# Moving the first image's token preparation of layer 1 into layer 0's last twelve units, and reordering the last units of layer 3

## The chip, the cores and the metric

The kernel runs on one core of one Trainium2 chip. The metric is the device time of one launch in microseconds (us). The core has a matmul engine (PE, TensorE), three engines for elementwise work (DVE is VectorE, ACT is ScalarE, POOL is GpSimd) and SP, whose queue issues the DMAs. Each engine works through a queue of its own and meets the others at semaphores. Matmul results are written to PSUM[...]; everything else is in SBUF.

## The reference

Four residual layers work one after the other on a float32 tensor of 4 images of 56 x 56 pixels and 256 channels. Ahead of each layer stands a group normalisation over 32 groups of 8 channels.

```python
x = x + L0(gn(x))   # 7x7 neighbourhood attention with zero padding, 8 heads of 32
x = x + L1(gn(x))   # attention over all 3136 tokens of an image, one head
x = x + L2(gn(x))   # 7x7 neighbourhood attention, half the heads dilated by (1, 2)
x = x + L3(gn(x))   # shifted 7x7 window attention with bias table
```

The change deals with the start of layer 1, which is this:

```python
xn = x / jnp.maximum(jnp.linalg.norm(x, axis=-1, keepdims=True), EPS)
A = jnp.einsum('bnc,cc,bmc->bnm', xn, W_adj, xn)
A = jnp.exp(5.0 * (A - jnp.max(A, axis=-1, keepdims=True)))
A = A * (1.0 - jnp.eye(n, dtype=A.dtype))
A = A / jnp.maximum(jnp.sum(jnp.abs(A), axis=-1, keepdims=True), EPS)
...
xW = jnp.einsum('bnc,dc->bnd', x, W_aff)
...
diff = rowsum * (xW + b_aff) - AxW
```

So each token is needed in two forms: scaled to unit length (for A) and multiplied by W_aff (for xW). `W_adj` is diagonal in use: einsum's `cc` takes its diagonal.

## The kernel before

All tensors lie channels first: 128 partitions hold one half of the channels, `CC` = 2 halves. The layers run one after the other, each with its own memory pools (`run`, L2213). Odd layers take their memory from the right side of SBUF, even ones from the left, so that a layer's first tiles can be loaded while the layer before still runs. A tile that takes the place of an older one waits for the older one's last users.

*Layer 0* (`layer0`, L1135) cuts each image into 8 bands of 7 rows (32 bands in all, numbered r from 0 to 31) and each band into 4 tiles, so it has 128 units, which `attend_pairs` (L1054) runs. A unit has logits on PE (L1067), a mask added on DVE (L1074) or multiplied on POOL (L1078), exponentials on ACT (L1075, L1077), sums of pairs on POOL (`both`, L1087), products on PE (`products`, L1096), and at its end a reciprocal and a scaling on DVE (`finish`, L1242 to L1249). The products of a unit run after the logits of the next one. Between logits and products stands the unit's `fill`: other work that is spread over the units by hand. In most bands it is the projection of rows of later chunks (`project_rows`, L1184: values, keys, queries); one band late comes the out projection with the residual add (`project_out`, L1266). The rows run out in band 28; bands 29, 30 and 31, the last twelve units, have only the out projections of bands 28, 29 and 30. That of band 31 follows after the last unit (L1315). The input pool `brief` (chunks of x, normalised chunks, v and also the queries q) is used until the row projections end.

Within layer 0 the order of each engine's instructions is made by a scheduler, with its own estimates of when data is there; in layer 1 PE's and DVE's order is that of the program, in layer 3 that of all four computing engines.

*Layer 1* (`layer1`, L1329) has 3136 tokens for each image: 24 tiles of 128 and a rest of 64 tokens. Its token preparation works by chunks of four tiles (`tokens`, L1361; six chunks, and a seventh for the rest): load from the stream in memory (L1372); normalise, on DVE (L945); square, on ACT (L1382); lengths, matmuls against a column of ones (L1392), then maximum on DVE (L1394), power -1/2 on POOL (L1395) and a diagonal matrix on POOL (L1403); values, x times W_aff on PE (L1414), moved out of PSUM by ACT or DVE by turns (`evac`, L956); unit length, a matmul of ones with the diagonal (L1424) and a product on DVE into `xnT` (L1426). For the rest chunk POOL also makes `xdr` (L1430). For image 0 all of that runs at the start of layer 1, by itself (`fresh`, L1662 to L1674); for the later images it runs in small steps within the attention of the image before. After it come the "rest" units (`rest_logits`, L1488, `rest_products`, L1515) and the main units (`logits`, L1445, `products`, L1547). In the rest products ACT copies half of the PSUM results into `acc` (L1485).

`layer2_ahead` (L1763) loads layer 2's weights and bias and takes the exponential of half of the bias on ACT (six steps, L1781). In the program it stands late in layer 1, but the scheduler may put it early on ACT and SP.

*Layer 3's end* (L2187 to L2207) is written out by hand. `u3` and `u4` are the last two units, `held` is the one before. `logits(w, between)` (L1014) runs `between` after POOL's product and ahead of DVE's mask. `last_row` (L2138) does the out projection of the last row of windows in two halves: it adds its own products (L2152) to x from PSUM directly (L2159). After it `unsafe` (L2236) sums the `watch` tiles (L2242), in which sums were collected through the kernel, tests them against bounds, and writes a flag (L2250), on which the program branches into a slower, safer version of itself. POOL adds reciprocals to a watch tile (`seen`, L993).

Of the kernel before, what the change touches and what calls it, by code (L numbers as in the profile page):

```python
# [24 lines left out]
FP = mybir.dt.float32  # L25
I32 = mybir.dt.int32
AF = mybir.ActivationFunctionType
# [803 lines left out]
def direct_blocks(ctx: ExitStack, tc: tile.TileContext, d: dict, watch):  # L831
# [302 lines left out]

    def layer0(early, big, pool, brief):  # L1135
        types, width = tile_types()
        xs, looks = {}, {}

        def load(r, held=xs, tag="x"):
# [8 lines left out]

        q = {(0, i): brief.tile([P, CC, BT], FP, tag="q", name="q0", bufs=6) for i in range(3)}
        for r in (3, 4, 5, 6, 0, 1, 2):  # L1150
# [5 lines left out]
        known(0, 0)  # L1156
        wv, wk, wq = (weight(big, n, C) for n in ("wv0", "wk0", "wq0"))
        late_loads()
# [25 lines left out]
        def project_rows(r):  # L1184

            b, g = divmod(r, NCH)
            xn = xns.pop(r)
            at = left(g, CH)
            v = brief.tile([P, 4, C], FP, tag="v", name="v0", bufs=1)

            def values(a):
                value_tiles(v, a, g, CH, xn, wv, bv0, vd[b])

            def keys(m):
                pm = project(wk, m * P, lambda h: xn[:, h, at:at + CH], CH)
                rows = pm.rearrange("p (r c) -> p r c", c=S)
                for i in range(NTC):
                    c0, n = key_range(*COLS[i:i + 2])
                    dst = (kE if i in (0, NTC - 1) else kI)[:, m, i // 2, 8 * g:8 * (g + 1), :]
                    nc.scalar.activation(dst, rows[:, :, c0:c0 + n], AF.Identity, bias=bk0[:, m:m + 1])  # L1200

            def queries(m):
                pm = project(wq, m * P, lambda h: xn[:, h, at:at + CH], CH)
                y = 8 * g
                while y < 8 * (g + 1):
                    i, y1 = y // TR, min((y // TR + 1) * TR, 8 * (g + 1))
                    if (b, i) not in q:
                        q[b, i] = brief.tile([P, CC, BT], FP, tag="q", name="q0", bufs=6)
                    nc.scalar.activation(q[b, i][:, m, (y - TR * i) * S:(y1 - TR * i) * S],
                                         pm[:, (y - 8 * g) * S:(y1 - 8 * g) * S],  # L1210
                                         AF.Identity, bias=qbias[:, 0, m:m + 1], scale=SCALE)
                    y = y1

            return [lambda f=f, m=m: f(m) for f in (values, keys, queries) for m in range(2)]
# [64 lines left out]
        def stream():  # L1279
# [10 lines left out]
            for r in range(NIMG * NB0):  # L1290
# [4 lines left out]
                steps.append(lambda r=r: [load(i, looks, "xs") for i in look_at.get(r + 1, [])])  # L1295
                if r:
                    at = (len(steps) + 2) // 2
                    steps[at:at] = project_out(r - 1)
# [4 lines left out]
                attns[r] = pool.tile([P, CC, BT], FP, tag="attn", name="attn0")  # L1303
                yield from spread([pair(r, t) for t in range(NTC)], steps)

        for r in range(3):
# [3 lines left out]
            if r < 2:  # L1310
                for step in project_rows(r):
                    step()
        check_sizes(pool)
        attend_pairs(pool, stream())
        for step in project_out(NIMG * NB0 - 1):  # L1315
            step()
# [11 lines left out]

    def layer1(early, big, pool, late, next_layer):  # L1329


        NB, REST = divmod(T, P)
        NC4 = NB // 4
        nonlocal m_bufs
        m_bufs = 1
        w_aff = weight(early, "waff", C)
        acc = big.tile([P, NB, C + 1], FP, name="acc")
        racc = big.tile([P, C + 1], FP, name="racc")
        xnT = big.tile([P, CC, (NB + 1) * P], FP, name="xnT")
        xw = big.tile([P, NB + 1, C + 1], FP, name="xw")  # L1340
        xdr = big.tile([P, CC, P], FP, name="xdr")
        shares = dram.tile([NIMG, (NB + 1) * P], FP, name="shares")
# [15 lines left out]
        nc.vector.tensor_scalar(offd, ident, -1.0, 1.0, ALU.mult, ALU.add)  # L1358
        nc.vector.memset(xw[:, :, C:], -1.0)

        def tokens(b, c, ps_a=ps_m):  # L1361
# [3 lines left out]
            n = m * P  # L1365
            by_dma = b > 0 and c in (0, 1, 2, NC4)
            box = {}
# [10 lines left out]
            def normal(h):  # L1378
                normalise(box["x"][:, h, :n], box["x0"][:, h, :n], known(1, b), h)
                if h:  # L1380
                    sq = box["x0"]
                    nc.scalar.activation(sq[:, :, :n], box["x"][:, :, :n], AF.Square)  # L1382
                    if b:
                        nc.gpsimd.tensor_tensor(sq[:, 0, :n], sq[:, 0, :n], sq[:, 1, :n], ALU.add)

            def lengths():
                pm, sq = ps_a(), box["x0"]
                rn = early.tile([P, 4, 1], FP, tag="rn", name="rn")
                halves = range(1 if b else CC)
                for i in range(m):  # L1390
                    for h in halves:
                        nc.tensor.matmul(pm[:, i:i + 1], lhsT=sq[:, h, i * P:(i + 1) * P], rhs=ones[:, 0:1],  # L1392
                                         start=(h == 0), stop=(h == halves[-1]))
                nc.vector.tensor_scalar_max(rn[:, :m, 0], pm[:, :m], TINY * TINY)  # L1394
                nc.gpsimd.tensor_tensor(rn[:, :m, 0], rn[:, :m, 0], mhalf[:, 0:1].to_broadcast([P, m]), ALU.pow)  # L1395
                box["share"] = early.tile([P, 4, P], FP, tag="dg", name="dg", bufs=1)
                if by_dma:
# [4 lines left out]
                else:  # L1402
                    nc.gpsimd.tensor_tensor(  # L1403
                        box["share"][:, :m, :], ident.rearrange("p (o q) -> p o q", o=1).to_broadcast([P, m, P]),
                        rn[:, :m, :].to_broadcast([P, m, P]), ALU.mult)
                    if b:
                        small.append((done + 2, unit_length, (b, c)))

# [22 lines left out]

            steps = [lambda i=i: values(i) for i in range(0, m, 2)]
            steps = [no_step] * 2 + [lengths] + steps if b else steps + [lengths, unit_length]
            return [load], [lambda h=h: normal(h) for h in range(CC)], steps

# [216 lines left out]
        for b in range(NIMG):  # L1652
            if b == 0:
                units += [(b, None, q) for q in range(2)]
            for j in range(NB):
# [3 lines left out]
                if b + 1 < NIMG and 0 <= j - 20 < 2:  # L1659
                    units.append((b + 1, None, j - 20))  # L1660
        turn = iter(range(6 * (NC4 + 1)))
        fresh = [tokens(0, c, lambda: psum_tile(*(("v", 2), ("o", 2), ("t", 1), ("s", 2))[next(turn) % 4])) for c in range(NC4 + 1)]  # L1662
        for c in range(2):
            fresh[c][0].pop()()
        for step in fresh[0][1] + fresh[0][2][-2:-1]:
            step()
        for c in range(NC4 + 1):
            *make, _, scale = fresh[c][2]
            ahead = fresh[c + 1] if c < NC4 else ([], [], [])
            for step in ahead[1] + make + ahead[2][-2:-1]:  # L1670
                step()
            scale()
            if c + 2 <= NC4:
                fresh[c + 2][0].pop()()  # L1674
        small, done = [], 0
# [107 lines left out]

    def layer2(held, big, pool, brief, last_steps):

# [223 lines left out]
    def layer3(early, big, pool, brief):  # L2009
# [128 lines left out]
        def last_row(r):  # L2138
# [4 lines left out]
            def first():  # L2143
                pair = psum_tile("o", 1, 2)
                for m in range(CC):
                    pms.append(pair[:, m, :WC])
                    half(m, 0)
                    nc.scalar.activation(x[:, m, :], x[:, m, :], AF.Identity, bias=bp3[:, m:m + 1])
# [6 lines left out]
            def second():  # L2155
                for m in range(CC):
                    half(m, 1)
                    for w, xv in parts(pms[m], x[:, m, :]):
                        nc.vector.tensor_tensor(xv, xv, w, ALU.add)  # L2159
                    transfer(4, r, x, 1, slice(m, m + 1))  # L2160
# [30 lines left out]
        out = project_out(r - 2)  # L2191
        logits(u3, done)
        out[0]()
        products(held)
# [16 lines left out]
    E = mybir.EngineType  # L2211

    def run(l, layer, fixed, kinds):  # L2213

# [11 lines left out]

    run(0, lambda own: layer0(*own), None, range(4))
    with pool_of(2, 0) as early, ExitStack() as ends:
        late = ends.enter_context(pool_of(1, 3))
        held = {}  # L2230
        last_steps = run(1, lambda own: layer1(*own, late, lambda: layer2_ahead(early, held)), {E.PE, E.DVE}, range(3))
        run(2, lambda own: layer2(held, *own, last_steps), None, range(1, 4))
    run(3, lambda own: layer3(own[1], own[0], *own[2:]), {E.PE, E.DVE, E.Activation, E.Pool}, (1, 0, 2, 3))


def unsafe(tc, pool, watch, flag):  # L2236

# [3 lines left out]
    for i, w in enumerate(watch):  # L2241
        nc.vector.tensor_reduce(t[:, i:i + 1], w, AX.X, ALU.add)  # L2242
    nc.vector.tensor_tensor(t[:, :n], t[:, :n], t[:, :n], ALU.mult)
# [60 lines left out]
def _build(arrays):  # L2304
# [6 lines left out]
    with tile.TileContext(nc) as tc:  # L2311
        with tc.tile_pool(name="flag", bufs=1) as pool:
            flag = pool.tile([1, 1], I32, name="flag")
            with tc.tile_pool(name="watch", bufs=1) as wp:
                watch = [wp.tile([P, n], FP, name=f"watch{n}") for n in (WC, 2 * CC + 2, 4 * NIMG * 8, 2 * NIMG * NB0 * NTC)]
                for w in watch:
                    nc.vector.memset(w, 0.0)
                direct_blocks(tc, d, watch)
                unsafe(tc, wp, watch, flag)
            again = nc.values_load(flag)  # L2320
# [13 lines left out]
```

## Time and profile before

| what | us |
|---|---|
| runs of the kernel | 3801.8, 3807.6, 3809.7 |
| median of these | 3807.6 |
| the profiled execution: its own time | 3789.3 |
| the profiled execution: span from the first to the last instruction | 3787.5 |
| PE busy | 3672.9 (97%) |
| POOL busy | 1811.6 (48%) |
| first logits of layer 0's last twelve units, on PE | 641.4 |
| end of layer 0's last products, on PE | 692.8 |
| out projection of band 31, on PE | 695.6 to 699.8 |
| fresh tokens of layer 1: first and last matmul | 703.3, 750.6 |
| first rest logits of layer 1, on PE | 752.2 |
| last residual add of layer 3, on DVE | 3777.7 |
| flag written, on DVE | 3778.2 |

The profile is of one execution. PE, PEld (weight loads), DVE, ACT and POOL are engines; L1414 is line 1414 of the kernel. A table by stretches of time gives for each stretch its length, then for each engine its busy time and number of instructions, then the clock that PE was granted (1.00 is full speed), the DMA engines' share and GB/s. A list of waits gives who waited for whom, then the total in us, the number of times and the longest. In the chain of waits each line is a start, a duration and what ran. "Idle before" is the time in which the engine stood still just ahead of an instruction, with the one that released it. A busy PE is modelled: waits shorter than what it has in flight can lie within its busy time.

### The profile page before, as it was taken

The page shows a single profiled execution, that of the slowest core. Times are in us where ns is not written, and L with a number is a line of the kernel's source. Part 1 is how long each engine was busy: PE and PEld are TensorE (multiplying, and loading weights), DVE is VectorE, ACT ScalarE, POOL GpSimd, SP SyncE. Part 2 cuts the span into 40 slices and gives each one's busy share as a digit, 9 for nine tenths or more (in the row PEclk, how much of TensorE's full clock was granted, in tenths as well). Part 3 has the DMA queues.
Part 4 walks back from the last instruction along what each step waited for, and adds up shares of the span by engine and source line. Part 5 has one row for each costly group of instructions (what it writes and reads, how often), then busy time and mean ns, then how long its engine had stood idle before and what let it go on. Part 6 is the DMA issues. An engine that isn't in the chain of part 4 may idle for free.

```text
span 3787.5 us, 112437 instructions
## 1 busy us (share of the span) xinstructions
PE 3672.9 (97%) x48876; PEld 2486.9 (66%) x48876; DVE 2201.7 (58%) x4195; ACT 1463.2 (39%) x3111; POOL 1811.6 (48%) x1966
## 2 busy tenths in 40 slices
PE   8999999899999999999999999999999999899998
PEld 4555566567777677766777767776666666555554
DVE  5776777534445444454444544446677777776776
ACT  5566565322222222222222222222666666444443
POOL 4777778512235222352222421123777777555555
PEclk9999999899999999999999999999999999999999
DMA  6544443400010100001001000002544443534443
GB/s 211 169 150 133 133 129 114 150 7 23 20 22 27 32 19 16 22 27 32 19 11 24 28 20 10 10 11 79 142 132 130 133 132 117 159 125 139 132 134 95
DMA packets 278039, 304.94 MB, mean 81 GB/s; under 512 B 33624, under 2 KB 268764, under 8 KB 277084
## 3 DMA queue, kind: packets, MB, share of 16 engines
q1 hardware_dynamic: 275680, 297.43, 25.9%
q8 instruction: 385, 6.31, 0.7%
q0 software_dynamic: 1568, 0.16, 0.1%
q14 instruction: 118, 0.97, 0.1%
q10 hardware_dynamic: 288, 0.08, 0.0%
HBM read 205.04 MB, written 92.55 MB: 79 GB/s over the span
## 4 chain that ended last, share of the span: by engine, by line
PE 87%; DVE 7%; POOL 2%; ACT 2%; issue 1%; DMA 1%; SPq 0%; DVEq 0%; ACTq 0%; POOLq 0%
PE ps_m L952 17%; PE ps_o L1555 14%; PE ps_s L1450 13%; PE ps_v L1560 13%; PE ps_m L979 7%; PE ps_o L1096 5%; PE ps_s L1067 5%; PE ps_t L1541 3%; PE ps_o L1036 2%; PE ps_s L1020 1%; PE ps_m L1414 1%; POOL b L1087 1%; DVE e L1074 1%; DVE rs L1247 1%; PE ps_v L1521 1%
## 5 line engine op out<-in xcount | busy, mean ns | idle before, releaser
L1482 DVE TENSOR_TENSOR acc<-acc,ps_v 128x257 f32<-128x257 f32 x1104 | 464.0, 423 | 781.9 <-PE ps_v L1560 752.4
L1560 PE MATMUL ps_v<-xw,e 128*128 128x257 f32 x2208 | 611.3, 381 | 3.4 <-DVE xnT L1426 2.2
L1555 PE MATMUL ps_o<-xw,at 128*128 128x257 f32 x2208 | 609.2, 380 | 0.0
L1450 PE MATMUL ps_s<-xnT,xd 128*128 128x512 f32 (+3 forms) x1344 | 571.6, 548 | 3.9 <-DVE xnT L1426 3.9
L1544 ACT COPY at<-ps_t 128x512 f32<-128x512 f32 (+3 forms) x332 | 170.3, 513 | 961.0 <-PE ps_t L1541 960.7
L1560 PEld LDWEIGHTS ps_v<-xw,e 128*128 128x128 f32 x2208 | 414.4, 190 | 143.6 <-issue 83.1
L1087 POOL TENSOR_TENSOR b<-e 126x336 f32<-126x336 f32 (+5 forms) x512 | 495.1, 988 | 7.8
L1555 PEld LDWEIGHTS ps_o<-xw,at 128*128 128x128 f32 x2208 | 419.9, 190 | 59.2
L952 PE MATMUL ps_m<-xn,w_wqkv 128*32 128x392 f32 x4096 | 376.2, 496 | 6.0 <-ACT gst L917 3.9
L1443 POOL TENSOR_SCALAR xd<-xnT,vec 128x128 f32<-128x128 f32 x192 | 116.5, 616 | 479.1 <-PE ps_s L1450 478.8
L1453 ACT ACTIVATE e<-ps_s 128x512 f32<-128x512 f32 x336 | 185.3, 552 | 356.2 <-PE ps_s L1450 352.9
L1078 POOL TENSOR_TENSOR e<-e,m0t 126x672 f32<-126x672 f32 (+3 forms) x128 | 238.5, 1864 | 170.1 <-ACT e L1077 167.3
L1450 PEld LDWEIGHTS ps_s<-xnT,xd 128*128 128x128 f32 x1344 | 225.8, 191 | 141.1 <-issue 126.0
L1078 POOL TENSOR_TENSOR e<-e,bias 119x784 f32<-119x784 f32 (+5 forms) x128 | 240.6, 1880 | 157.8 <-ACT e L1077 157.4
L1096 PEld LDWEIGHTS ps_o<-e,vp 124*32 124x32 f32 (+3 forms) x8192 | 200.0, 110 | 102.8 <-issue 81.2
L998 ACT ACTIVATE no<-rs 128x168 f32<-128x168 f32 (+2 forms) x256 | 94.0, 367 | 433.2 <-DVE rs L1892 191.7
L952 PEld LDWEIGHTS ps_m<-xn,w_wqkv 128*32 128x32 f32 x4096 | 124.4, 110 | 180.0 <-issue 128.1
L1892 DVE RECIPROCAL rs<-ps_o 128x196 f32<-128x196 f32 (+2 forms) x128 | 175.7, 1373 | 111.0 <-PE ps_o L1096 108.9
L1096 PE MATMUL ps_o<-e,vp 124*32 124x112 f32 (+3 forms) x8192 | 232.2, 249 | 4.5 <-POOL e L1078 3.8
L1075 ACT ACTIVATE e<-e 126x672 f32<-126x672 f32 (+5 forms) x256 | 219.6, 858 | 13.3 <-DVE e L1074 1.1
L1077 ACT ACTIVATE e<-ps_s 126x672 f32<-126x672 f32 (+5 forms) x256 | 205.9, 804 | 0.6 <-PE ps_s L1067 0.6
L979 PE MATMUL ps_m<-w_wqkv,xn 128*32 128x256 f32 x3136 | 197.8, 383 | 3.1 <-DVE v L983 2.4
(212 smaller groups left out, 5942.3 us busy)
## 6 DMA issues: line engine op xcount, KB each, us to landing
x<-xr SPq DMA_DIRECT2D x64, 392.0 KB
x<-in_x SPq DMA_DIRECT2D x53, 448.0 KB
x<-x SPq DMA_DIRECT2D x60, 392.0 KB
xr<-x SPq DMA_DIRECT2D x60, 392.0 KB
vd<-v SPq DMA_DIRECT2D x72, 256.0 KB
xr<-in_x SPq DMA_DIRECT2D x32, 392.0 KB
xr<-x SPq DMA_DIRECT2D x28, 448.0 KB
x<-xr SPq DMA_DIRECT2D x28, 448.0 KB
```

What stands on the lines that cost most here:

```text
L952: nc.tensor.matmul(pm[j * HD:(j + 1) * HD, :n], lhsT=w[:, h, col + j * HD:col + (j + 1) * HD], rhs=rhs(h), start=(h == 0), stop=(h == CC - 1))
L979: nc.tensor.matmul(pm[i:i + HD, j * C:(j + 1) * C], lhsT=xn[:, h, first + i:first + i + HD], rhs=w[:, h, :], start=(h == 0), stop=(h == CC ...
L1067: nc.tensor.matmul(s[j // 2][:nk, j % 2, (2 * i + u) * nq:(2 * i + u + 1) * nq], lhsT=k(j, u), rhs=q(j), start=True, stop=True)
L1075: nc.scalar.activation(ev, ev, AF.Exp)
L1077: nc.scalar.activation(ev, sv, AF.Exp)
L1078: nc.gpsimd.tensor_tensor(parts(ev), parts(ev), w["emask"], ALU.mult)
L1087: nc.gpsimd.tensor_tensor(w["b"][a][:nk, :, :2 * nq].rearrange("p h (i c) -> p h i c", i=2), ev[:, :, :, 0, :], ev[:, :, :, 1, :], ALU.add)
L1096: nc.tensor.matmul(w["o"](k, i)[j * HD:(j + 1) * HD], lhsT=ones[:nk, :HD] if k else v(j, u), rhs=w["b"][j // 2][:nk, j % 2, i * nq:(i + 1) ...
L1450: nc.tensor.matmul(s[:, :n], lhsT=xd[j][:, h, :], rhs=xnT[:, h, first * P:last * P], start=(h == 0), stop=(h == CC - 1))
L1482: nc.vector.tensor_tensor(acc[:, i, :], acc[:, i, :], pv[:, :C + 1], ALU.add)
L1555: nc.tensor.matmul(out[j][:, :C + 1], lhsT=e[:, col(i)] if i == j else at[:, col(i)], rhs=xw[:, i, :], start=(i == j), stop=(i == NB - 1))
L1560: nc.tensor.matmul(pv[:, :C + 1], lhsT=e[:, col(i)], rhs=xw[:, j, :], start=True, stop=True)
```

## The change

The fresh tokens of image 0 are no longer made at layer 1's start. A new function `first_tokens` makes the same as steps, which are put into the fills of layer 0's last twelve units by a plan written by hand (`ALONE` = band 29), with a thirteenth step group after the last unit. At that point layer 0's pool `brief` is closed, and `xnT`, `xw` and `xdr` are taken from the right side, in the memory that it leaves; for that the queries move to the pool `early`, and the three projection weights to `brief`. Tokens are loaded straight into `xnT` and normalised, squared and scaled there in place. Normalising is done by ACT (`normalise_act`, L941) instead of DVE; the two halves of the squares are added by DVE ahead of the lengths, so that these are one matmul for each tile instead of two. All PSUM tiles of these steps are `ps_m` (two banks), where before they went round v, o, t and s. In the last three bands the out projection of the band before stands in the fills of the band's second and third tiles. `w_aff` is loaded into a pool that is opened early.

In layer 3 the out projection's first step of the last but two row moves into the slot between POOL's product and DVE's mask of `u3`; the two halves of `last_row` get separate PSUM tiles; and the sums of `unsafe` are ordered behind the last residual add.

```diff
-    def layer0(early, big, pool, brief):
+    def layer0(early, big, pool, begin_layer1):
+        passing = ExitStack()
+        brief = passing.enter_context(pool_of(0, 3))
...
-        q = {(0, i): brief.tile([P, CC, BT], FP, tag="q", name="q0", bufs=6) for i in range(3)}
+        q = {(0, i): early.tile([P, CC, BT], FP, tag="q", name="q0", bufs=6) for i in range(3)}
...
-        wv, wk, wq = (weight(big, n, C) for n in ("wv0", "wk0", "wq0"))
+        wv, wk, wq = (weight(brief, n, C) for n in ("wv0", "wk0", "wq0"))
...
-                if r:
+                if 0 < r < ALONE:
                     at = (len(steps) + 2) // 2
                     steps[at:at] = project_out(r - 1)
...
-                yield from spread([pair(r, t) for t in range(NTC)], steps)
+                if r < ALONE:
+                    yield from spread([pair(r, t) for t in range(NTC)], steps)
+                    continue
+                if r == ALONE:
+                    passing.close()
+                    tokens.extend(begin_layer1())
+                out = project_out(r - 1)
+                for t in range(NTC):
+                    w = pair(r, t)
+                    w["fill"] = lambda steps=tokens.pop(0) + (out[t - 1:t] if t else []): [f() for f in steps]
+                    yield w
...
+        ALONE, tokens = NIMG * NB0 - 3, []
         attend_pairs(pool, stream())
-        for step in project_out(NIMG * NB0 - 1):
+        for step in tokens.pop(0) + project_out(NIMG * NB0 - 1):
             step()
...
+    def first_tokens(few, keep, brief):
+        w_aff = weight(few, "waff", C)
+        xnT = keep.tile([P, CC, (NB + 1) * P], FP, name="xnT")
+        xw = keep.tile([P, NB + 1, C + 1], FP, name="xw")
+        xdr = keep.tile([P, CC, P], FP, name="xdr")
...
+        def normal(c):
+            m, n, x = part(c)
+            sq = box["sq"] = brief.tile([P, CC, 512], FP, tag="sq", name="sq1")
+            for h in range(CC):
+                normalise_act(x[:, h], x[:, h], known(1, 0), h)
+            nc.scalar.activation(sq[:, :, :n], x, AF.Square)
+            nc.vector.tensor_tensor(sq[:, 0, :n], sq[:, 0, :n], sq[:, 1, :n], ALU.add)
+        def lengths(c):
...
+            for i in range(m):
+                nc.tensor.matmul(pm[:, i:i + 1], lhsT=box["sq"][:, 0, i * P:(i + 1) * P], rhs=ones[:, 0:1], start=True, stop=True)
+            nc.vector.tensor_scalar_max(rn[:, :m, 0], pm[:, :m], TINY * TINY)
+            nc.gpsimd.tensor_tensor(rn[:, :m, 0], rn[:, :m, 0], mhalf[:, 0:1].to_broadcast([P, m]), ALU.pow)
+            nc.gpsimd.tensor_tensor(dg[:, :m, :], ident.rearrange("p (o q) -> p o q", o=1).to_broadcast([P, m, P]),
+                                    rn[:, :m, :].to_broadcast([P, m, P]), ALU.mult)
...
+        v0, v2 = lambda c: values(c, 0), lambda c: values(c, 2)
+        R = NC4
+        plan = [
+            [(load, R), (load, 0)],
+            [(load, 1), (normal, R)],
+            [(load, 2), (lengths, R), (normal, 0)],
+            [(load, 3), (v0, R), (unit_length, R), (lengths, 0)],
+            [(v0, 0), (normal, 1), (v2, 0)],
+            [(load, 4), (unit_length, 0), (lengths, 1)],
+            [(v0, 1), (normal, 2)],
+            [(load, 5), (v2, 1), (unit_length, 1), (lengths, 2)],
+            [(v0, 2), (normal, 3), (v2, 2)],
+            [(unit_length, 2), (lengths, 3)],
+            [(v0, 3), (normal, 4)],
+            [(v2, 3), (unit_length, 3), (lengths, 4), (normal, 5)],
+            [(v0, 4), (v2, 4), (unit_length, 4), (lengths, 5), (v0, 5), (v2, 5), (unit_length, 5)]]
...
-        fresh = [tokens(0, c, lambda: psum_tile(*(("v", 2), ("o", 2), ("t", 1), ("s", 2))[next(turn) % 4])) for c in range(NC4 + 1)]
...
             def first():
-                pair = psum_tile("o", 1, 2)
-                for m in range(CC):
-                    pms.append(pair[:, m, :WC])
+                for m, tag in enumerate(("o", "s1")):
+                    pms.append(psum_tile(tag, 1, 2)[:, 0, :WC])
...
-        logits(u3, done)
-        out[0]()
+        logits(u3, lambda: (out[0](), done()))
...
-        nc.vector.tensor_reduce(t[:, i:i + 1], w, AX.X, ALU.add)
+        with tc.issue_after(last):
+            nc.vector.tensor_reduce(t[:, i:i + 1], w, AX.X, ALU.add)
```

In the program the plan's step groups stand unit by unit. In the built order the scheduler has moved some of them: the seven loads are issued in the first units of band 29, and all of ACT's normalising steps stand before the exponentials of band 29's fourth unit.

## The prediction

> **What bounds the kernel now.** I read the page's engine shares first (PE 97% of the span of 3787.5 us), then the tables by stretch of time round the seam between layers 0 and 1, then the list of waits there, then the chain of waits and the timeline of the last 25 us. The kernel as a whole is bound by PE, so a change pays only where PE waits, runs at a low clock, or does work that goes away. All three meet at the seam. The twelve last units of layer 0 run from their first logits on PE at 641.4 us to 692.8; layer 1's "rest" logits, the first matmuls after the fresh tokens, start at 752.2.
>
> ```profile
> core 0: us, PE busy (x) PEld busy (x) DVE busy (x) ACT busy (x) POOL busy (x), PEclk, DMA share, GB/s
> 657.00:673.00 16.00, 13.27 (x366) 9.26 (x356) 13.54 (x19) 8.11 (x16) 15.25 (x13) 1.00 0.36 114
> 682.00:684.00 2.00, 1.75 (x48) 1.29 (x47) 1.97 (x3) 0.70 (x3) 1.81 (x3) 0.50 0.88 299
> 689.00:705.00 16.00, 9.39 (x160) 5.49 (x152) 9.57 (x18) 1.98 (x5) 3.18 (x3) 0.89 0.28 80
> 705.00:721.00 16.00, 15.90 (x73) 12.70 (x73) 5.82 (x11) 3.29 (x4) 11.07 (x13) 0.83 0.79 296
> 721.00:737.00 16.00, 13.30 (x63) 10.52 (x62) 5.18 (x9) 8.68 (x10) 4.58 (x5) 0.85 0.63 248
> ```
>
> The first row is one band (four units) near layer 0's end: POOL is busy 15.25 of 16 us and PE 13.27, so POOL sets the pace there. The waits say the same, and the rows below show what the fresh tokens cost after it:
>
> ```profile
> PE ps_o L1096 <- POOL b L1087: 6.5, 10, 1.1
> ...
> PE ps_v L1392 <- ACT x L1382: 3.5, 1, 3.5
> ...
> PE ps_m L952 <- DVE attn L1249: 2.8, 1, 2.8
> PE ps_s L1392 <- ACT x L1382: 2.7, 1, 2.7
> ...
> PE ps_s L1492 <- POOL xdr L1430: 1.6, 1, 1.6
> ```
>
> In the seam PE waits 3.5 us for the first squares, 2.8 us for the last attention rows, 2.7 us behind ACT's bias exponentials and 1.6 us for xdr; and its granted clock lies between 0.83 and 0.89 for 48 us, with single stretches at 0.50. The end of the kernel is a chain of small steps:
>
> ```profile
> 3773.17 0.98 POOL watch L993
> ...
> 3774.17 0.57 DVE bounds L2242
> ...
> 3775.26 0.70 DVE xr L2159 x3
> 3775.97 0.04 issue
> 3776.01 0.91 PE ps_o L2152 x8
> ...
> 3777.01 0.70 DVE xr L2159 x3
> ```
>
> A check sum (L2242) waits for POOL ahead of the last residual adds, and the last eight matmuls wait for the first adds, though they write the other bank of the same tile.
>
> [...] 0.50 at 682 to 688 us, after the stretch 675 to 680 with PE busy 3.54 of 5 us. [...] the square at 726.29 stood behind three bias exponentials (2.91 us) while PE waited 2.7 us for it. [...] At the seam the trace has up to 476 GB/s (708 to 712 us), in the last units 114 GB/s.
>
> **The change part by part.**
>
> 1. *Token work moves into the units.* At full clock one chunk of four tiles takes PE 6.46 us now (from 735.34 to 741.80: lengths 1.81, unit length 0.94, values 1.73 and 1.98). The new lengths use one half instead of two (DVE adds the squares first), half of 1.81, so a chunk takes 5.55. Built, the order of instructions has in band 29 (first of the three) only the small rest chunk and chunk 0's lengths; in bands 30 and 31 two chunks' worth each, 11.1 us; and behind the last products chunk 4's values and unit length, all of chunk 5 but its weights, then the last out projection.
>
> 2. *Band 29* (four units, 16.0 us now). POOL gets 0.55 + 0.40 (pow, diagonal of the rest chunk) and 1.19 (xdr): 15.25 + 2.14 = 17.4. ACT gets all the normalising that DVE did, twelve steps of 128x512, and the built order puts every one of them before the exponentials of this band's fourth unit. The price is in the groups by shape:
>
> ```profile
> L942 ACT ACTIVATE xn<-x,gst 128x392 f32<-128x392 f32 x64 | 41.9, 703 | 1.8 <-PE ps_m L979 1.8
> L942 ACT ACTIVATE xn<-x,gst 128x448 f32<-128x448 f32 x56 | 39.5, 762 | 9.3 <-POOL gst L926 9.3
> ```
>
> 56 columns more cost 59 ns, so 512 columns are some 0.83 us (on DVE it was 0.51): 10.0. With two squares (2.1), the rest chunk (1.25), its copy (0.37) and ACT's own 8.55 this is 22.3 us: ACT becomes the bound of band 29. Its first loads wait until the last row projection has read the closed pool (PE, 640.6 us); the later ones stand behind v gathers on SP, which waited at most 2.2 us for PE. I take 23 us; low 21.5 (one step slips into the next band), high 27 (1 us of waiting in each unit).
>
> 3. *Bands 30 and 31.* PE: 13.3 by its busy row, 11.4 if the waits that are inside it are taken out (4 logits of 1.06, products of 1.27 and 1.0 twice each, out projection 2.66), plus 11.1: 22.5 to 24.4; I take 23.5. POOL: 15.25 + two to three times 2.06 (pow 1.02, diagonal 1.04) = 19.4 to 21.4. DVE: 13.54 + 2 x (square add 0.5, copy 0.69, unit length 1.22, maximum 0.16) = 18.7. ACT: 8.1 + 2 x (1.06 + 0.59) = 11.4. So PE becomes the bound. That it can run without gaps beside such a POOL the trace shows at 560 to 590 us: PE 30.00 of 30 us with POOL at 25.89. High bound 28 per band, if queues in order cost 1 us per unit.
>
> 4. *Sum for the seam.* From 641.4: 23 for band 29; 7/4 x 23.5 = 41 to the last unit's logits; 8.2 to the end of its products (684.66 to 692.81 now); tail 3.5 + 0.94 + 0.9 + 3.5 + 0.94 + 2.7 = 12.5, and 1 for evacuations between two banks of ps_m: 13.5. The rest logits start at 727.1 instead of 752.2: 25.1 us gained. xdr is early, the bias exponentials are no longer in front of squares.
>
> 5. *What is late next.* In ACT's new order six bias exponentials (0.97 us each) stand in the first rest products, between the copies that free ps_v. There PE is at four pairs of 1.28 us; with up to two exponentials ahead of each copy I reckon 2.2 us lost. Their 3 MB load now follows the last row of layer 0 on SP; issue to use was within 18 us before and the load ran at over 400 GB/s, so it lands some 11 us after the rest logits start and ACT asks after 12: no wait, or 4 us if late. Low 0, high 6. PE has only 11.4 + 2.4 us of work in band 29's 23, so I expect its clock to fall once and band 30 to start slow: 2, between 0 and 6. Seam net: 25.1 - 2.2 - 2 = 20.9.
>
> 6. *Layer 3's end.* The out projection's ACT step now precedes an exponential, so ps_m comes free 2.6 us earlier (PE waited 2.64 at 3761.49). DVE's four reciprocals of 2.61 us take most of that back: the last one can start at about 3767.9 instead of 3769.2, gain 1.3. Two separate tiles free the last matmuls (2.6 us wait) and the check sums go behind the adds (1.3 wait and 0.9 busy): the last add ends near 3773.7 instead of 3777.7. But then all four sums (0.16, 0.29, 0.35, 0.56), three small steps and the flag follow: flag at 3776.2 instead of 3778.2. The branch waits for the flag: 2.0 gained, between 0 and 4 (if only the last output DMA counted). The two sums that leave the middle of layer 3 are 0.5 us of DVE beside PE: nothing. The w_aff load at the start: 256 KB, nothing, at worst 0.5.
>
> Total 20.9 + 2.0 = 22.9, taken as 23: the profiled execution of 3789.3 us (span 3787.5) would be 3766. The median of the runs is 3807.6, 18 above that execution; the same 23 gives **3785**.
>
> **Rivals.** *A, full overlap:* PE never waits in bands 30 and 31: 21.5 + 1.75 x 22.5 + 7.5 + 12 = 80.4, rest logits at 721.8, gain 30.4, no loss at exponentials or clock, 3 at the end: 3774. For it: the gapless stretch at 560. Against: POOL, DVE and PE would all be over 80% busy at once. *B, queues in order eat half:* 27 + 1.75 x 25.5 + 9 + 15 = 95.6, rest logits at 737, gain 15; less 4 for exponentials and clock, 2 at the end: 3795. For it: each token step crosses four engines, and ps_m has two banks for projections, lengths, values and unit lengths. *C, slower:* normalising steps wait in ACT's queue for loads that wait on SP behind gathers, and hold back the exponentials, POOL's products and so PE, unit after unit. The price is what a unit loses; from 31 us in all (23 plus 0.2% of the time, 7.6), 2.6 us in each of twelve units, it makes the kernel slower; at 3.5 us, 3808 - 23 + 42 = 3827. Against: SP's longest wait for PE there is 2.2 us, and the loads all lie in the first band. *D, nothing to measure:* a loss between B and C. That the work does not move at all is excluded by the built order.
>
> **How the numbers follow.** Forecast (gain 15 to 29, 3779 to 3793) 0.60; A 0.15; B (gain 8 to 15) 0.14; D 0.06; C 0.05. The range of 3774 to 3796 leaves out half of A's better side, a little of B, and D and C, some 2 in 10. What a measurement of this kernel can tell from no change is about 0.2%, 7.6 us: faster 0.89, same 0.06, slower 0.05.
>
> **What would show it.** Right: rest logits near 727 us; band 29 near 23 us with ACT over 90% busy; PE over 95% busy in the two bands after, with POOL near 85%; clock 1.0 from early in band 30; bias exponentials among the acc copies with PE losing about 2 us; last residual adds back to back, then four sums, flag 2 us earlier. Wrong: ACT waiting for a DMA in band 29 by several us, PE waiting for ps_m copies or for ACT's exponentials by over 1 us per unit in bands 30 and 31, or a clock of 0.5 through a whole band.

## The result, and the profile after

| what | before | after |
|---|---|---|
| median of six executions each, us | 3804.8 | 3769.3 |
| their range, us | 3801.1 to 3809.7 | 3765.6 to 3771.8 |
| the profiled execution, its own time, us | 3789.3 | 3769.9 |
| its span, us | 3787.5 | 3768.0 |

The measured ratio is 0.9905, with an interval of 0.9892 to 0.9918: 35.5 us gained where 23 were forecast, and 3769 lies below the range of 3774 to 3796. Of the 16 us between 3785 and 3769, 3 are the median that the forecast started from (3807.6 for 3804.8). A second comparison (in the second group of experiments below) gave 0.9913 (0.9895 to 0.9930). Between the two profiled executions the difference is only 19.4 us. So two questions stand: why the ordinary executions gained some 14 to 16 us more than the profiled ones, and whether the 19.4 came about as worked out.

The table by stretches of the kernel after, from the first of layer 0's last twelve units on (columns as before: length, then busy time and instructions by engine, PE's granted clock, DMA share, GB/s):

```profile
core 0: us, PE busy (x) PEld busy (x) DVE busy (x) ACT busy (x) POOL busy (x), PEclk, DMA share, GB/s
641.00:657.00 16.00, 12.79 (x285) 8.38 (x280) 10.43 (x16) 12.14 (x22) 11.82 (x9) 0.89 0.87 256
657.00:673.00 16.00, 13.82 (x203) 11.21 (x196) 9.88 (x16) 12.52 (x22) 11.32 (x12) 0.79 0.47 144
673.00:689.00 16.00, 15.74 (x301) 11.66 (x300) 12.55 (x19) 5.92 (x13) 14.91 (x13) 1.00 0.20 61
689.00:705.00 16.00, 15.51 (x288) 11.75 (x289) 12.02 (x18) 8.08 (x13) 14.15 (x11) 1.00 0.24 68
...
640.00:770.00 130.00, 120.53 (x1555) 81.72 (x1548) 75.85 (x122) 62.81 (x116) 76.58 (x72) 0.96 0.40 132
```

From 673 us on PE is busy 98% and 97% of the stretch: there the moved work is packed as tightly as PE allows. In the first two rows nobody is: ACT, the forecast's bound, is busy 76% and 78%. The timeline of PE (start, duration, what ran, and in brackets the idle time ahead with its releaser) at the starts of bands 29, 30 and 31 and of the rest logits:

```profile
643.41 1.13 PE L1067 MATMUL ps_s<-q,kE 32*124 32x112 f32 x32
...
649.38 1.11 PE L1067 MATMUL ps_s<-q,kI 32*126 32x84 f32 x28 [2.53 <-ACT e L1077]
...
667.42 2.01 PE L1067 MATMUL ps_s<-q,kE 32*124 32x112 f32 x32
...
692.49 1.02 PE L1067 MATMUL ps_s<-q,kE 32*95 32x112 f32 x32
...
732.31 1.94 PE L1574 MATMUL ps_s<-xnT,xdr 128*64 128x512 f32 x8 [0.75 <-DVE xr L1275]
```

Band 29 takes 24.0 us, band 30 25.1, and from band 29's first logits to the rest logits it is 88.9 us (110.8 before). The waits in the same stretch say what band 29 met:

```profile
ACT xnT L942 <- DMA xnT<-x: 4.0, 4, 1.8
...
PE ps_s L1067 <- ACT e L1077: 2.5, 1, 2.5
...
PE ps_o L1096 <- POOL b L1087: 1.4, 2, 1.1
PE ps_m L1380 <- DVE xnT L1400: 1.3, 1, 1.3
```

ACT's first normalising step stands ahead of an exponential and waits 1.8 us for its load; PE stands still 2.5 us for that exponential. PE's waits for POOL's sums have fallen from 6.5 us to 1.4. At the end of the kernel DVE now runs, in its timeline:

```profile
3755.29 0.69 DVE L2226 TENSOR_TENSOR xr<-xr,ps_o 128x343 f32<-128x343 f32 x3 [1.04 <-ACT xr L2215]
3755.96 0.69 DVE L2226 TENSOR_TENSOR xr<-xr,ps_s 128x343 f32<-128x343 f32 x3
3756.57 1.14 DVE L2323 TENSOR_REDUCE bounds<-watch 128x1 f32<-128x392 f32 x4
...
3758.67 0.15 DVE L2331 TENSOR_SCALAR flag<-n_safe 1x1 int32<-1x1 f32 x1 [0.37 <-PE n_safe L2330]
```

The last adds are back to back and the four sums follow, as forecast.

### The profile page after: what moved, and what is told of

Same layout as the page of the kernel before. It is cut to its first block, busy times and chain, and to the rows that moved or that the text cites. A ratio compares the mean times of both kernels' runs of the same rounds, so it can differ in the third digit from the quotient of the medians.

```text
span 3768.0 us, 112324 instructions
## 1 busy us (share of the span) xinstructions
PE 3665.8 (97%) x48826; PEld 2478.1 (66%) x48826; DVE 2200.9 (58%) x4188; ACT 1472.2 (39%) x3125; POOL 1815.9 (48%) x1966
```

## The experiments

Times are medians; ratios are against the kernel before, run on the same chip in turn, with 95% intervals.

### Where before's time goes in an ordinary execution; the two halves of the change

Four kernels: before unchanged; the change without its layer 3 edits; before with those edits alone; and before with the bias exponentials held back:

```diff
-            nc.scalar.activation(part, part, AF.Exp)
+            with tc.issue_after(latest_at[0].ins):
+                nc.scalar.activation(part, part, AF.Exp)
```

(`latest_at` is ACT's newest copy of a main unit's transposed block at the point where the program builds the exponentials, which is late in layer 1: in this kernel's trace they run from 1993.7 us on, where before had them from 723.5.)

> The kernel before, unchanged, for a profile at its ordinary time. Theory L (a stall near the seam that the profiled execution of before happened to escape, some 15 us of its ordinary time): the new profile has a time of 3801 to 3810, and against the earlier profile (span 3787.5) some 15 us more lie in one place between 640 and 800 us, where something waits for a DMA or for ACT's bias exponentials. Rival M (a general drift: clock or DMA a little slower everywhere): the 15 us are spread over layers 0, 2 and 3 in proportion, no place has more than 5. Rival N (the profiled execution is always shorter than the timed ones): the profile is again near 3788 while the timed runs stand at 3801 to 3810.

> The change without its three edits in layer 3. By the sum on record the seam is worth 20.9 and the end 2.0: 2 us slower than the whole change, 3771 beside 3769. Theory L (the extra gain belongs to the seam): 3771 or a little below. Rival E (the extra 12 to 15 us come from layer 3's end, where order is now pinned): 3781 to 3786.

> The kernel before with the three layer 3 edits alone. Sum on record: 2.0 faster, 3803. Theory L: 3803 (0 to 4 faster). Rival E: 12 to 17 faster, 3788 to 3793.

> The kernel before with one edit: layer 2's six bias exponentials on ACT (6 x 1.03 us, and whatever they wait for) may not start before layer 1's first main unit, so the fresh token stage no longer has them in ACT's queue. Theory L with the exponentials as the culprit (they stand in order before squares and wait for a 3 MB load): 15 to 18 us faster, 3787 to 3790. Rival L2 (the stall lies in the token loads or elsewhere): only the 2.7 us wait of PE behind them and a little clock go, 2 to 5 faster, 3800 to 3803. Rival M or N: the same 2 to 5.

| kernel | median, us | ratio |
|---|---|---|
| before again | 3801.9 | 1.0006 (0.9999 to 1.0013) |
| seam only | 3772.1 | 0.9932 (0.9919 to 0.9946) |
| end only | 3796.0 | 0.9987 (0.9979 to 0.9995) |
| before, exponentials late | 3795.9 | 0.9992 (0.9984 to 1.0001) |

The seam carries most; the end is worth about 5 us (2 to 8) alone, and beside the seam 3 by the medians, more by the ratios. The traces are closer: from layer 3's first logits to the last matmul the six profiles without these edits take 491.8 to 494.4 us, the ten with them 489.3 to 489.6. The exponentials are not the culprit: their wait went, with at most 6 us. Rival N falls too, as the new profile of before was taken at 3803 us (span 3801.2). Neither theory L nor rival M fits the 13.7 us against the earlier profile: 4.0 lie between band 29's start and the rest logits (114.8 us for 110.8), and most of the others in layer 2, which the change leaves alone. At the seam PE has the same waits, within 0.3 us. What differs is the clock. Stretches of the earlier profile of before:

```profile
640.00:770.00 130.00, 110.54 (x1500) 75.31 (x1492) 71.26 (x113) 48.60 (x91) 73.86 (x70) 0.92 0.39 133
...
700.00:710.00 10.00, 6.75 (x31) 5.89 (x32) 3.14 (x9) 2.70 (x3) 2.88 (x3) 0.83 0.79 255
```

and of the new one:

```profile
640.00:770.00 130.00, 110.75 (x1480) 77.09 (x1471) 70.62 (x111) 47.42 (x88) 73.62 (x69) 0.88 0.39 133
...
700.00:710.00 10.00, 6.51 (x30) 5.60 (x23) 3.64 (x10) 2.11 (x2) 2.15 (x2) 0.62 0.51 151
```

In these records the clock is either full or half, so a mean of 0.92 over 130 us is 2 x 0.08 x 130 = 21 us at half clock; 0.88 is 31, and the kernel after, with 0.96, has 10. The records give the lengths as 20.5, 30.7 and 10.2 us, each a multiple of 3.41. The same program, with the same waits, got another number of such stretches in each of the two executions. Each execution's mean clock is recorded beside its span, and over 109 executions of before, made beside all the experiments, it orders them:

| mean granted clock | executions | median span, us |
|---|---|---|
| 0.989 | 4 | 3806.0 |
| 0.990 | 12 | 3803.0 |
| 0.991 | 36 | 3801.2 |
| 0.992 | 33 | 3797.8 |
| 0.993 | 21 | 3794.5 |
| 0.994 | 1 | 3790.1 |
| 0.995 | 2 | 3787.8 |

The profile that the prediction was worked out from had 0.994 at 3787.5: such a good one comes 3 times in 109. A line through the 109 gives 0.36 us of span for each us at half clock. Layer 2, where no edit reaches, says the same in the traces: over the sixteen profiles it takes 645.0 us with 3.4 at half clock and 652.4 with 17.1, a line through them 0.42 us for each. That is a relation and not yet a cause.

### Is it a cause? Useless work for PE, and where the normalising stands

If the low clock is a cost of PE's gaps, work that does nothing must make the kernel before faster. Fifteen matmuls whose result nobody reads, put into its three gaps:

```diff
+        pm = ps_m()
+        for i in range(n):
+            nc.tensor.matmul(pm[:, :C], lhsT=ones, rhs=w[:, 0, :], start=True, stop=True)
...
+        with tc.issue_after(last_product[0].ins):
+            keep_busy(wo, 5)
...
+        keep_busy(w_aff, 7)
...
+        keep_busy(w_aff, 3)
```

Beside it the changed kernel again, and two with its normalising on DVE, wholly or for one half of the channels:

```diff
-                normalise_act(x[:, h], x[:, h], known(1, 0), h)
+                normalise(x[:, h], x[:, h], known(1, 0), h)
```

```diff
+                (normalise, normalise_act)[h](x[:, h], x[:, h], known(1, 0), h)
```

> The changed kernel, unchanged, beside the kernel before on the same chip. Theory K (clock: before loses at the seam several stretches of 3.4 us at half clock, more of them in an ordinary execution than in the profiled one, and the change removes most of them; across executions of before the span goes up by some 0.39 us for each us at half clock): 3767 to 3771, spread about 6 us, mean granted clock 0.995 beside 0.992 of before. Rival U (before's long time came from something that is not the clock and that differs from chip to chip): gain anywhere between 20 and 36, clock no guide.

> The kernel before with fifteen useless matmuls (128x256, 0.46 us each at full clock, 6.9 us in all) in PE's three gaps at the seam: 5 ahead of band 31's out projection (gap 2.8 us), 7 ahead of the first lengths (gap 3.5), 3 ahead of the rest logits (gap 1.6). Theory K: PE stays busy, the half clock stretches between 690 and 765 us go from 20 to 31 us down to about 10, and the kernel becomes 4 to 8 us faster although PE does more. Rival U (waits alone count): the work fills the gaps and nothing changes, 0 to 2 slower; rival S (the low clock comes from something other than idle time): 2 to 4 slower, the half clock stretches stay.

> The changed kernel with all normalising of the moved tokens on DVE (0.51 us for 128x512) instead of ACT (0.75 to 0.8). Theory A (ACT's normalising makes band 29 24 us long): ACT's load in the band falls by some 10 us, DVE's rises by 6 to 20; band 29 takes 20 to 21 us, and PE's low clock after it shrinks; 3 to 6 us faster, 3763 to 3766. Rival Q (band 29 is set by waits for the loads and by queues in order, not by ACT's load): the loads now hold DVE's masks and reciprocals instead; 0 to 4 slower.

> The changed kernel with one half of the channels normalised on DVE and the other on ACT. Theory A: ACT and DVE each have some 17.5 us of work in band 29, so POOL and PE set it at 19 to 20 us; 4 to 7 us faster, 3762 to 3765. Rival Q: both queues wait for the loads, no gain, 0 to 3 slower.

| kernel | median, us | ratio | mean clock, all executions |
|---|---|---|---|
| before, beside these | 3803.0 | 1 | 0.991 |
| changed, again | 3769.5 | 0.9913 (0.9895 to 0.9930) | 0.995 |
| before with useless matmuls | 3792.6 | 0.9977 (0.9969 to 0.9985) | 0.994 |
| changed, normalising on DVE | 3774.1 | 0.9927 (0.9909 to 0.9944) | 0.994 |
| changed, one half on DVE | 3773.1 | 0.9926 (0.9908 to 0.9945) | 0.994 |

The useless matmuls made the kernel 9 us faster (6 to 12), a little over what theory K said; rivals U and S had it the same or slower. PE's timeline in before again, then theirs (the trace has two records for each useless matmul), and their stretch of 130 us:

```profile
696.20 4.24 PE L952 MATMUL ps_m<-attn,w_wo 128*32 128x392 f32 x32 [2.78 <-DVE attn L1249]
703.92 3.58 PE L1392 MATMUL ps_v<-ones,x 128*128 128x1 f32 x16 [3.49 <-ACT x L1382]
...
756.80 2.52 PE L1492 MATMUL ps_s<-xnT,xdr 128*64 128x512 f32 x8 [1.57 <-POOL xdr L1430]
```

```profile
694.43 4.02 PE L1059 MATMUL ps_m<-w_wo,ones 128*128 128x256 f32 x10
698.38 2.84 PE L952 MATMUL ps_m<-attn,w_wo 128*32 128x392 f32 x32
701.97 3.29 PE L1059 MATMUL ps_m<-w_waff,ones 128*128 128x256 f32 x14 [0.75 <-DVE xr L1280]
705.10 1.84 PE L1401 MATMUL ps_v<-ones,x 128*128 128x1 f32 x16
...
752.07 2.52 PE L1501 MATMUL ps_s<-xnT,xdr 128*64 128x512 f32 x8 [0.28 <-POOL xdr L1439]
```

```profile
640.00:770.00 130.00, 115.25 (x1552) 79.30 (x1540) 72.70 (x115) 50.03 (x94) 74.38 (x71) 0.96 0.39 134
```

The out projection after the first five and the lengths after the next seven run at once and in less time: 2.84 us for 4.24, and 1.84 for 3.58. The clock over the seam is 0.96, that of the changed kernel. From band 29's first logits to the rest logits this kernel takes 109.1 us for 114.8 in before again, with more work for PE.

Both DVE variants missed what theory A said: they did not gain 3 to 7 us but seem to lose 4 to 5, as rival Q had it, though the intervals overlap. Band 29 took 27.6 us with everything on DVE and 26.5 with half, and PE waits 3.1 us in one piece for a DVE mask in both. The timelines of the first, DVE above and POOL below, show when a step that took 0.5 us in before takes longer here:

```profile
649.29 3.28 DVE L945 TENSOR_SCALAR xnT<-xnT,gst 128x512 f32<-128x512 f32 x2
654.38 0.45 DVE L945 TENSOR_SCALAR xnT<-xnT,gst 128x512 f32<-128x512 f32 x1
668.90 2.27 DVE L945 TENSOR_SCALAR xnT<-xnT,gst 128x512 f32<-128x512 f32 x1
...
648.93 2.08 POOL L1078 TENSOR_TENSOR e<-e,m0t 124x896 f32<-124x896 f32 x1 [3.22 <-ACT e L1077]
651.10 2.46 POOL L1087 TENSOR_TENSOR b<-e 124x448 f32<-124x448 f32 x2
668.79 2.10 POOL L1078 TENSOR_TENSOR e<-e,m0t 124x896 f32<-124x896 f32 x1 [1.89 <-ACT e L1077]
```

With POOL idle the step takes 0.45 us. Started 0.1 us behind a POOL product it takes 2.27 and ends 0.3 us after that product. What holds it back is not shown. The twelve steps took 1.1 us each in the mean, so ACT at 0.81 us was the cheaper engine here.

### What makes band 29 long; the exponentials; useless work elsewhere

In the next two kernels each normalising step of the changed kernel, with its squares, is tied behind the exponential of the unit in whose fill the plan has it; the second also holds the bias exponentials back, and a third does only that:

```diff
-                normalise_act(x[:, h], x[:, h], known(1, 0), h)
...
+            with tc.issue_after(newest_exp[0].ins):
+                for h in range(CC):
+                    normalise_act(x[:, h], x[:, h], known(1, 0), h)
```

> The changed kernel with the moved normalising steps and squares on ACT tied behind the exponentials of the unit in whose fill the plan puts them, so that none of them stands in front of band 29's first exponentials. Theory W (band 29 takes 24 us not because ACT has too much work, but because its first normalise waits 1.8 to 2.1 us for a load ahead of an exponential, PE stands still 2.5 to 2.8 us behind it, and the clock is then halved for 6.8 to 10 us in bands 29 and 30): the wait goes, band 29 takes 18 to 20 us, bands 30 and 31 21.5 to 23.5 each, at most one half clock stretch is left; 5 to 8 us faster, 3761 to 3765. Theory A (ACT's total load sets the band): the same load is spread over three bands, so band 29 falls to 19 and bands 30 and 31 rise by as much, 0 to 2 faster.

> As the kernel with the normalising tied to its units, and the six bias exponentials of layer 2 in addition held back behind layer 1's first main units. If they cost PE what the sum on record said (2.2 us, in the rest products, where they stand between copies that free ps_v): 2 us faster than that kernel, 3759 to 3763. If what PE lost there was hidden: the same.

> The changed kernel with the bias exponentials held back alone. Sum on record: 2.2 us faster, 3767; if hidden, or if they cost as much where they go: 3769.

Then the same tie, but for all steps to the exponential of band 29's first unit (`box["exp"]`), without and with the bias exponentials held back; and before with the fifteen useless matmuls in layer 1's twenty-first unit (`if k == 20: keep_busy(w_aff, 15)`) in place of the gaps.

> The changed kernel with its moved normalising steps held back behind the exponentials of band 29's first unit only; behind that they may run as early as the loads allow, so that band 29 still does all of them but one. Theory V (both held together: ACT must not wait for a load ahead of an exponential, and the normalising must be early, because squares that come late make PE wait for ps_m in bands 30 and 31): PE's 2.5 to 2.8 us wait goes with some of the half clock behind it, bands 30 and 31 stay as in the changed kernel: 3 to 5 us faster, 3764 to 3767. Theory A (ACT's load sets band 29): the wait moves to the next exponential, 3769.

> The same with layer 2's six bias exponentials held back behind layer 1's first main units in addition. If their cost of about 1 to 2 us in the rest products is real and adds up: 3762 to 3766, the fastest; if not: as without.

> The kernel before with the same fifteen useless matmuls (6.9 us at full clock), but all in layer 1's twenty-first unit, where PE is busy without a gap. Theory K (in the seam they paid by keeping the clock up): here there is no clock to win, the kernel becomes 6 to 8 us slower, 3808 to 3811. Rival R (they changed something else, such as the order or memory of the program, that makes it faster): no slower or even faster.

| kernel | median, us | ratio |
|---|---|---|
| tied to its units | 3776.2 | 0.9932 (0.9915 to 0.9949) |
| the same, exponentials late | 3771.8 | 0.9920 (0.9901 to 0.9938) |
| changed, exponentials late | 3768.2 | 0.9911 (0.9893 to 0.9928) |
| behind the first exponential | 3769.3 | 0.9914 (0.9897 to 0.9930) |
| the same, exponentials late | 3767.8 | 0.9909 (0.9892 to 0.9925) |
| before, useless matmuls elsewhere | 3805.2 | 1.0013 (1.0004 to 1.0021) |

The useless matmuls in a full place cost 5 us (2 to 8), in the gaps they gained 9. Their trace has the seam at 114.8 us, as in before again, and layer 1 longer by 6.0. So it is not their mere being in the program that gains.

Tying each step to its unit did in band 29 what theory W said and failed as a whole. PE's timeline at the starts of bands 29, 30, 31 and the rest logits, then two of its waits after band 29:

```profile
642.69 1.13 PE L1069 MATMUL ps_s<-q,kE 32*124 32x112 f32 x32
...
662.01 1.82 PE L1069 MATMUL ps_s<-q,kE 32*124 32x112 f32 x32
...
690.37 1.02 PE L1069 MATMUL ps_s<-q,kE 32*95 32x112 f32 x32
...
735.64 1.94 PE L1577 MATMUL ps_s<-xnT,xdr 128*64 128x512 f32 x8 [0.75 <-DVE xr L1277]
```

```profile
PE ps_m L952 <- DVE xnT L1403: 3.3, 2, 1.6
PE ps_m L1383 <- DVE xw L959: 2.3, 2, 2.1
```

Band 29 fell from 24.0 to 19.3 us, but band 30 rose from 25.1 to 28.4 and the rest from 39.8 to 45.3: 93.0 in all. PE now waits for the two banks of `ps_m` that DVE empties late; in the changed kernel the first of these waits is 0.7 us after band 29. Early normalising, which makes band 29 long, pays itself back. (The seam is 4 of the 7 us that this kernel lost.) Behind the first exponential the 2.5 us wait is gone from PE and another stands in its place, 2.2 us for `attn` on DVE; the band takes 22.3, the seam 88.4 for 88.9, and the time is the same. Theory V had hoped for 3 to 5.

The bias exponentials held back gave 1.3, 1.5 and 4.4 us in the three pairs, all of one sign and none outside its interval; the first pair was not measured side by side. The traces place the gain: from the rest logits to its last matmul, layer 1 is 1.0 to 1.9 us shorter in each of these pairs. The fastest median, 3767.8, cannot be told from the changed kernel's.

## Why the prediction was wrong, and where it was right

**The step that failed is the clock in part 5, and with it the total's last line.** Part 5 charged an estimated 2 us for the low clock that the changed kernel keeps. The low clock that goes away has no term of its own: part 4 counts the new work at full clock and takes before's seam as one profile had it, so it holds the 20.5 us at half clock of that execution. The last line then carries "the same 23" over to the median. But that execution was among the best. It spent 44 us of its span at half clock and the profiled one of the changed kernel 42, so between them there is no clock to win: 19.4. In ordinary executions before has a mean clock of 0.9916, which is 2 x 0.0084 x 3799 = 64 us at half clock; the changed kernel, over its second set, has 0.9952 and 36 us. At 0.36 us for each, 28 us fewer are worth an estimated 10; at the full half, 14, and 19 to 25 of the 33 to 35.5 are left. That the clock is low where the gaps are was in the prediction's opening (0.83 to 0.89 for 48 us), with no price; the 18 us between the profile and the median were noticed, and not asked about.

The traces place this by stretches. "Before again" and "changed, again" are the second profiles, of ordinary executions; in brackets are the us at half clock:

| stretch, us | before | changed | before again | changed, again |
|---|---|---|---|---|
| to band 29's first logits | 641.4 (3.4) | 643.4 (10.2) | 642.0 (3.4) | 640.5 (3.4) |
| from there to the rest logits | 110.8 (20.5) | 88.9 (10.2) | 114.8 (30.7) | 89.0 (10.2) |
| layer 1 from there | 1888.7 (3.4) | 1889.3 (0) | 1889.1 (3.4) | 1889.1 (0) |
| layer 2, to layer 3's first logits | 645.1 (6.8) | 647.4 (13.7) | 652.4 (17.1) | 650.2 (17.1) |
| layer 3, to the last matmul | 492.0 (0.9) | 489.6 (0) | 493.5 (3.7) | 489.6 (0) |

In the first pair the seam with layer 1 gained 21.3 us where 20.9 were worked out, and layer 3 2.4 where it was 2.0; the rest of the 19.4 is a loss of 4.3 in layer 0's earlier bands and layer 2, where no step was moved. In the second pair they gained 25.8 and 3.9, with 20.5 us less at half clock in the seam and 3.7 less in layer 3. So the sum held for the execution that it was made from. Of the 14 us by which the second pair gained more, 6 come from these two places and 8 from those other stretches, where the time changes from one execution to the next.

What starts a single stretch at half clock is not shown. In the profiles of before and after each is 3.41 or 6.83 us long (the one that runs past the last instruction apart). Why the same waits came with 20.5 us of it in one execution and with 30.7 in another is not shown either, as no run here moves a gap. One came without a long gap: before's clock fell to half at 681.3 us, after 675 to 680 with PE busy 3.54 us of 5, and the longest wait of PE in the 6 us ahead was 0.71 us. The useless matmuls show that gaps are the cause for before's seam (9 us gained; a clock of 0.96 there for 0.88). For the changed kernel the cause is inferred from its fewer gaps and its clock, as no run opened them again. Not settled: what makes those stretches differ so between executions.

Point by point, for the rest:

- *Part 1, PE's price of a chunk:* right. A chunk's lengths take 0.95 us in PE's timeline, half of the 1.84 to 1.95 before; its unit length is unchanged, 1.13 beside 1.10.
- *Part 2, band 29, 23 us:* 24.0, the size right and the reason half right. A normalising step costs 0.81 us (0.83 estimated), but ACT was busy 76%, not over 90%. It waited 4.0 us for loads, the sign that was named for "wrong", and the first two rows of the table of stretches hold 10 us at half clock.
- *Part 3, bands 30 and 31:* PE-bound as said, with POOL busier than forecast (93% and 88% in the rows from 673 us on, for 85%); 25.1 us for 23.5; band 30 begins in a half clock stretch (its first logits take 2.01 us, 1.13 at full clock), which lasts to 671.3 us and explains up to an estimated 2.
- *Part 4:* 88.9 us to the rest logits for 85.7; they came at 732.3 and not 727.1, also because band 29 began 2.0 us later in this execution, after 6.8 us of half clock at 484 us, where nothing was changed.
- *Part 5, exponentials:* 2.2 forecast, 1.0 to 1.9 in layer 1's traces. The load landed in time: ACT does not wait for it.
- *Part 6, the end:* right in the order and, in the first pair of profiles, in size. From the last but one logits to the flag, before took 22.3 us and the changed kernel, in its second profile, 19.9. What it left out is clock again: four of the six profiles without these edits have 3.4 us at half clock just behind a wait of 2.64 us that PE has for ACT, some 17 us before the flag; none of the ten with them has.
- *The rivals:* C did not come, though its first step did: ACT waited for loads ahead of an exponential, but PE stood still for it once, not unit after unit. A came nearest in time (3774), for a reason that did not hold: the overlap was not full, and the rest logits came at 732.3, not 721.8. That the total lands near A's is luck. B and D did not come.

## What to carry to other kernels

A profile is one draw: where the kernel has gaps in PE's work (here of 1.6 to 3.5 us), compare its granted clock with that of ordinary executions (here 0.994 and 0.9916) before a gain is worked out, and price the clock that a change wins as well as the waits it removes. Useless matmuls in a gap are a cheap test of whether the clock is what a gap costs, and the same ones in a full place the control (9 us gained and 5 lost here). And a step that is taken out of one engine's way arrives later for the next: count the seam as a whole (93.0 us for 88.9 when each step was tied to its unit), not the band (19.3 for 24.0).

## What the runs showed of the hardware

A DVE tensor-scalar of 128x512 float32 took 0.45 us alone and up to 2.27 beside a POOL product. Fifteen matmuls of 128x256 with no use cost 5 us in a full place and gained 9 in three gaps of 1.6 to 3.5 us. Half clock came in stretches of 3.41 and 6.83 us, and not only behind gaps of 1.6 to 3.5 us: before had it from 681.3 us on, with no wait of PE over 0.71 us in the 6 us ahead. Over 109 executions of one program the median span goes from 3788 to 3806 us with the mean granted clock from 0.995 to 0.989.
